# Two attention layers on one core: value products of two steps issued together, and a pool of eight for the weights

## The chip, the core and the metric

One core of a Trainium2 chip runs the whole program. The metric is device time in microseconds; lower is better. Engines are named as in the profile: PE is TensorE (matrix products), DVE is VectorE, ACT is ScalarE, POOL is GpSimd and SP issues most DMAs. Matrix products are written to PSUM, eight banks of 512 float32 columns on 128 partitions; the other engines read them there.

## The reference

The input x has two images of 256 channels and 64 x 64 positions, so 4096 tokens each. Two layers follow each other.

Layer 0 (4 heads of 16):

```python
xn = layernorm over channels(x) * norm_w + norm_b
q, k, v = split(einsum('bnc,oc->bno', xn, qkv_w))
attn = softmax(einsum('bhnd,bhmd->bhnm', q, k) * 16 ** -0.5)
dyn = conv2(relu(conv1(x)))                 # one factor for each query
out = einsum('bhnm,bhmd->bhnd', attn * dyn, v)
x = sigmoid(gamma * (out @ out_w.T) + x)
```

Layer 1 (4 heads of 64): queries, keys and values from x by 1 x 1 convolutions with bias, `softmax(q k / 8) v`, an output convolution with bias, plus x. The result is float32.

## The kernel before

**Preparation.** The first stretch of the program normalises x block by block (512 tokens), makes queries and keys as sums of three bf16 parts, the values in float32 (`vs0`, 32 columns for each head, the first of them ones, so that the value product also gives the sum of the weights) and `dyn`. Its tiles lie in pools (`own_prep`) that are closed before the loop.

**Layer 0's loop.** A unit is one image and a block of 512 queries; there are 16 units of 32 steps (`END0` = 512 steps). A step takes 128 keys against the unit's 512 queries, for 4 heads. The loop variable is t. Every instruction is issued through `seq`, which keeps the program's order on each engine, so the order written in the loop is the order on PE, ACT, DVE and POOL. A step issues, in this order:

- `weigh(t, 0)`: two score products s (L453) for heads 0 and 1, each followed by its exponential (L458, ACT), from a PSUM tile of one bank (`ps2`, three buffers) into half of a weight tile p (128 x 2 x 512 float32 in SBUF);
- `maxima(t + LEAD0, 1)`: two score products a (L407) for the queries of a later step, into a two-bank tile (`ps1`, two buffers), and one DVE reduction over them (L412). `LEAD0` is 35: the maxima of a unit are found while the unit before it is weighed, and are subtracted in the later products by three more rows of the operands;
- `weigh(t, 1)` and `maxima(t + LEAD0, 0)` for heads 2 and 3;
- `gather(t - 1)`: the value products av (L471) of the step before, four products with 32 columns each, one for each head, accumulated over the unit in one bank (`psa`, one buffer). At a unit's last step it also copies that bank to SBUF (L483, ACT);
- what is hung on this step: `fold` and `turn` (the maxima of the next unit are split and put into its queries, steps 28 to 30 of a unit; `turn` borrows a `ps1` tile for `nm`, L434, which ACT copies, L438), `send_sums`, `factor` and `scale_all` (1 over the sums, by way of DRAM), `project` (L555, borrows a `ps1` tile for o) and `add_x` (L560, DVE), `finish` and the loads.

Maxima stop where t + 35 reaches 512. From there on the tile of heads 0 and 1 is a pair from `ps1` with one exponential over both banks (L460), and layer 1's first keys, values and queries are made between the steps.

The weight tile comes from the pool `l0w`, which also holds queries and factors, with four buffers of its tag: two tiles for each step, so two steps. The name `l0p` does not exist. The pool `l0w` is opened ahead of the preparation's pools, so it lies below them.

**Layer 1** follows with its own pools once layer 0's are closed. Nothing in it is touched.

Of the kernel before, what the change touches and what calls it, by code (L numbers as in the profile page):

```python
# [8 lines left out]
F32 = mybir.dt.float32  # L9
# [6 lines left out]
P = 128  # L16
NB = 512
# [15 lines left out]
def conv_attention_kernel(  # L33
# [20 lines left out]
    B, _, N = x.shape  # L54
# [9 lines left out]
    own0 = ExitStack()  # L64
# [3 lines left out]
    l0w = own0.enter_context(tc.tile_pool(name="l0w", bufs=2))  # L68
# [91 lines left out]
    def later_load(t, src):  # L160
        nc.sync.dma_start(out=t, in_=src)
        return t

    def more_constants():

        gam = later_load(
            const.tile([P, 1], F32, tag="gam", name="gam"), gamma.partition_broadcast(P)
        )
        wo0 = const0.tile([P, C], F32, tag="wo0", name="wo0")
        nc.gpsimd.memset(wo0, 0.0)  # L170
        for h in range(H):
            later_load(
                wo0[32 * h + 1 : 32 * h + 1 + D0, :], out_wT[h * D0 : (h + 1) * D0, :]
            )
        return gam, wo0
# [39 lines left out]
    def hung(t, place):  # L215
        for step in extras.pop((t, place), []):
            step()
# [11 lines left out]
    END0 = len(units0) * NM  # L229
# [4 lines left out]
    with own0:  # L234
# [11 lines left out]
            seq(nc.gpsimd.memset(ones_at, 1.0))  # L246

        work, qs0, mxs, pts, avs, dyns, res, facts = {}, {}, {}, {}, {}, {}, {}, {}
        ks0, negs0 = {}, {}

        def bank_two(name):
            return pairs[0].tile([P, 2, NB], F32, tag="two", name=name)
# [145 lines left out]
        def maxima(x, g):  # L398

            u = b, j = units0[x // NM]  # L400
            m, i = divmod(x % NM, PB)
            if u not in mxs:
                mxs[u] = small.tile([P, PB * H, NJ], F32, tag="mx0", name=f"mx0_{b}_{j}")
            ps = bank_two(f"a0_{b}_{j}_{x % NM}_{g}")
            for k in range(2):
                h = 2 * g + k
                seq(nc.tensor.matmul(  # L407
                    ps[:, k, :], qs0[u][:RQ, h, bass.ts(i, P)], ks0[b, m][:RQ, h, :],
                    start=True, stop=True,
                ))  # L410
            h = i * H + 2 * g
            seq(nc.vector.tensor_reduce(mxs[u][:, h : h + 2, m], ps, AX.X, ALU.max))  # L412
# [27 lines left out]
        def weigh(t, g):  # L440
            u = b, j = units0[t // NM]
            m = t % NM
            pt = l0w.tile([P, 2, NB], F32, tag="p", bufs=4, name=f"p0_{b}_{j}_{m}_{g}")
            late = t + LEAD0 >= END0 and g == 0
            if late:
                two = bank_two(f"s0_{b}_{j}_{m}")
            for k in range(2):
                h = 2 * g + k
                if late:
                    ps = two[:, k, :]  # L450
                else:
                    ps = ps2.tile([P, NB], F32, tag="s", name=f"s0_{b}_{j}_{m}_{h}")
                seq(nc.tensor.matmul(  # L453
                    ps, ks0[b, m // PB][:RS, h, bass.ts(m % PB, P)], qs0[u][:RS, h, :],
                    start=True, stop=True,
                ))
                if not late:
                    seq(nc.scalar.activation(pt[:, k, :], ps, AF.Exp, scale=D0**-0.5))  # L458
            if late:
                seq(nc.scalar.activation(pt, two, AF.Exp, scale=D0**-0.5))  # L460
            pts[t, g] = pt

        def gather(t):


            u = b, j = units0[t // NM]
            m = t % NM
            if m == 0:
                avs[u] = psa.tile([P, NB], F32, tag="av", name=f"av0_{b}_{j}")
            for h in range(H):  # L470
                seq(nc.tensor.matmul(  # L471
                    avs[u][32 * h : 32 * h + 32, :],
                    vs0[b][:, m, 32 * h : 32 * h + 32],
                    pts[t, h // 2][:, h % 2, :],
                    start=(m == 0),
                    stop=(m == NM - 1),
                    skip_group_check=True,
                ))
            pts.pop((t, 0))
            pts.pop((t, 1))  # L480
            if m == NM - 1:
                a = l0w.tile([P, NB], F32, tag="avs", name=f"avs0_{b}_{j}")
                seq(nc.scalar.copy(a, avs[u]))  # L483
                avs[u] = a
# [118 lines left out]
        for n in range(len(blocks) + 3):  # L603
# [37 lines left out]
            if old is not None:  # L641
                prep_product(*old)
                prep_split(*old)
                b, j = old
# [20 lines left out]
        ps2 = own_psum.enter_context(tc.tile_pool(name="ps2", bufs=3, space=PSUM))  # L665
        psa = own_psum.enter_context(tc.tile_pool(name="psa", bufs=1, space=PSUM))
        pairs[0] = ps1
        gam, wo0 = more_constants()


# [83 lines left out]
        for t in range(-LEAD0 + NM, max(t for t, _ in extras) + 1):  # L754
            ahead = t + LEAD0
            hung(t, "start")
            if 0 <= t < END0:
                weigh(t, 0)
            if ahead < END0:
                maxima(ahead, 1)  # L760
            hung(t, "middle")
            if 0 <= t < END0:
                weigh(t, 1)
            if ahead < END0:
                maxima(ahead, 0)
            if 0 <= t - 1 < END0:
                gather(t - 1)
            hung(t, "end")
        assert not extras
# [23 lines left out]
    with (  # L793
# [468 lines left out]
        for n, u in enumerate(units):  # L1262
            b, g, j = u
# [142 lines left out]
        for t in range(max(t for t, _ in extras) + 1):  # L1406
            inside, behind = 0 <= t < END, 0 <= t - LAG < END
            pair = (2 * t, 2 * t + 1)
            scores = [score(pair[0])] if inside else []
            if 0 <= t - LAG - 1 < END:  # L1410
                weigh(pair[1] - 2 * LAG - 2)
            hung(t, "start")
            hung(t, "between")
            if inside:
                scores.append(score(pair[1]))
            hung(t, "early")
            if inside:
                keep(pair[0], scores[0])
            hung(t, "kept")
            if behind:  # L1420
                shift(pair[0] - 2 * LAG)
                weigh(pair[0] - 2 * LAG)
            hung(t, "early end")
            if inside:
                keep(pair[1], scores[1])
            if 0 <= t - LAG - 1 < END:
                for c in pair:
                    gather(c - 2 * LAG - 2)
                    if c - 2 * LAG - 2 == 2 * END - 2:
                        keep_late(1)  # L1430
            hung(t, "late")
            hung(t, "late end")
            if behind:
                shift(pair[1] - 2 * LAG)
            hung(t, "end")
# [67 lines left out]
```

## Time and profile before

| | |
|---|---|
| median of 3 runs | 4342.19 us (4340.53 to 4343.92) |
| profiled execution | 4343.31 us, span 4341.5 us, mean granted PE clock 0.99 |
| busy in the span | PE 95%, DVE 86%, ACT 79%, POOL 60% |
| layer 0's steps with value products | first av at 252.5 us, last at 1758.4 us |

The windows view gives busy time of each engine in a stretch, with the number of instructions in brackets. In the timeline each row has the start, the time until the last of the merged instructions ends, the engine, line, operation, output and inputs, and in square brackets the engine's idle time ahead of it with what ended that. A PE row's end is modelled and overlaps the next row, so the pace of PE is read from start to start. The value products are float32; a step's four of them leave eight records.

### The profile page before, as it was taken

How to read it: one execution, taken by the hardware profiler on the slowest of the kernel's cores; microseconds unless marked ns; L12 is line 12 of the kernel's file. 1: busy time of each engine (PE TensorE's matmuls, PEld its weight loads, DVE VectorE, ACT ScalarE, POOL GpSimd, SP SyncE). 2: the span in 40 equal slices, each digit the busy share in tenths (PEclk: the TensorE clock that was granted, in tenths of full speed). 3: DMA queues.
4: the chain of work that ended last, by engine and by line, in shares of the span. 5: the costliest groups of instructions: out<-in, count | busy, mean ns of one | idle time of the engine just before them, and what ended most of it. 6: DMA issues, size and time to landing. Idle time of an engine off the chain costs nothing. (4 is left out here: it accounts for less than half of the span.)

```text
span 4341.5 us, 56781 instructions
## 1 busy us (share of the span) xinstructions
PE 4120.8 (95%) x20650; PEld 1348.3 (31%) x20650; DVE 3725.2 (86%) x3417; ACT 3422.0 (79%) x4616; POOL 2584.8 (60%) x1456
## 2 busy tenths in 40 slices
PE   6899999999999999899999999999999999999998
PEld 3433333333333333333333333333333333222322
DVE  5778888888888883599999999999999999999997
ACT  2257777777777777698889888898898888988885
POOL 6600000010000000299999999999999999999995
PEclk8889999999999999999999999999999999999999
DMA  5400000010000002111112111112211112211213
GB/s 145 117 19 22 25 24 17 17 37 21 17 21 19 14 13 71 59 35 40 40 34 66 50 42 38 33 41 69 54 36 37 40 45 59 60 40 42 52 40 117
DMA packets 237521, 191.63 MB, mean 44 GB/s; under 512 B 155700, under 2 KB 168820, under 8 KB 237240
## 3 DMA queue, kind: packets, MB, share of 16 engines
q1 hardware_dynamic: 235384, 187.40, 16.2%
q8 instruction: 162, 2.65, 0.3%
q14 instruction: 119, 0.97, 0.1%
q10 hardware_dynamic: 1856, 0.59, 0.1%
HBM read 136.55 MB, written 51.38 MB: 43 GB/s over the span
## 5 line engine op out<-in xcount | busy, mean ns | idle before, releaser
L1027 POOL TENSOR_TENSOR acc<-acc,raw 128x1024 f32<-128x1024 f32 x821 | 1949.6, 2375 | 60.7 <-ACT raw L1015 9.3
L412 DVE TENSOR_REDUCE mx<-a 128x2 f32<-128x1024 f32 x1024 | 1209.1, 1221 | 252.5 <-PE a L407 248.2
L458 ACT ACTIVATE p<-s 128x512 f32<-128x512 f32 x1978 | 1023.4, 604 | 349.6 <-PE s L453 348.8
L931 DVE TENSOR_TENSOR rmax<-s,rmax 128x1024 f32<-128x1024 f32 x960 | 1172.7, 1222 | 139.9 <-PE s L914 128.6
L914 PE MATMUL s<-q,k 64*128 64x512 f32 x4096 | 1114.7, 636 | 105.7 <-ACT raw L932 101.3
L932 ACT COPY raw<-s 128x1024 f32<-128x1024 f32 x1024 | 1036.6, 1012 | 206.8 <-DVE rmax L931 109.8
L1003 DVE TENSOR_TENSOR raw<-raw,shift 128x1024 f32<-128x1024 f32 x961 | 1164.3, 1213 | 3.9 <-ACT shift L985 2.4
L1015 ACT ACTIVATE raw<-raw 128x1024 f32<-128x1024 f32 x1024 | 1086.6, 1062 | 78.7 <-DVE raw L1003 47.8
L1056 PE MATMUL av<-raw,v 128*64 128x512 f32 x4096 | 1008.9, 608 | 4.0 <-ACT raw L1015 2.5
L453 PE MATMUL s<-q,k 99*128 99x512 bf16 x2048 | 616.6, 381 | 15.4 <-ACT p L458 14.7
L407 PE MATMUL a<-k,q 96*128 96x512 bf16 x2048 | 612.0, 382 | 10.7 <-DVE mx L412 8.8
L471 PE MATMUL av<-p,v 128*32 128x512 f32 x4096 | 546.2, 605 | 0.2 <-ACT avs L483 0.2
L914 PEld LDWEIGHTS s<-q,k 64*128 64x128 f32 x4096 | 311.7, 185 | 707.2 <-ACT raw L932 525.6
L1056 PEld LDWEIGHTS av<-raw,v 128*64 128x64 f32 x4096 | 243.0, 136 | 651.8 <-issue 455.1
L453 PEld LDWEIGHTS <-k 99*128 99x128 bf16 x2048 | 160.8, 97 | 516.9 <-issue 390.5
L570 POOL TENSOR_SCALAR res<-res 128x1024 f32<-128x1024 f32 x16 | 16.7, 1044 | 498.1 <-ACT res L569 498.1
L407 PEld LDWEIGHTS <-q 96*128 96x128 bf16 x2048 | 200.8, 98 | 285.6 <-issue 56.5
L422 POOL CAST part<-neg 128x16 bf16<-128x16 f32 x16 | 3.4, 211 | 446.7 <-PE a L407 274.3
L519 POOL TENSOR_TENSOR f<-f,dyn 128x16 f32<-128x16 f32 x15 | 3.3, 221 | 371.8 <-DVE f L518 371.8
L1025 POOL TENSOR_TENSOR acc<-raw,raw 128x1024 f32<-128x1024 f32 x64 | 152.4, 2382 | 54.0 <-ACT raw L1015 54.0
L992 POOL TENSOR_TENSOR raw<-raw,row 128x1024 f32<-128x1024 f32 x63 | 152.2, 2417 | 39.0 <-DMA row<-neg 39.0
L471 PEld LDWEIGHTS av<-p,v 128*32 128x32 f32 x4096 | 80.9, 108 | 218.2 <-issue 210.2
(345 smaller groups left out, 2101.9 us busy)
## 6 DMA issues: line engine op xcount, KB each, us to landing
row<-neg SPq DMA_DIRECT2D x64, 512.0 KB
x<-in_x_dram SPq DMA_DIRECT2D x16, 512.0 KB
res<-in_x_dram SPq DMA_DIRECT2D x16, 512.0 KB
x<-res SPq DMA_DIRECT2D x16, 512.0 KB
att<-rows SPq DMA_DIRECT2D x62, 128.0 KB
kd<-part SPq DMA_DIRECT2D x96, 64.0 KB
qd<-part SPq DMA_DIRECT2D x96, 64.0 KB
k<-kd SPq DMA_DIRECT2D x16, 384.0 KB
```

The lines of the kernel that those rows point to most:

```text
L407: seq(nc.tensor.matmul(ps[:, k, :], qs0[u][:RQ, h, bass.ts(i, P)], ks0[b, m][:RQ, h, :], start=True, stop=True,))
L412: seq(nc.vector.tensor_reduce(mxs[u][:, h : h + 2, m], ps, AX.X, ALU.max))
L453: seq(nc.tensor.matmul(ps, ks0[b, m // PB][:RS, h, bass.ts(m % PB, P)], qs0[u][:RS, h, :], start=True, stop=True,))
L458: seq(nc.scalar.activation(pt[:, k, :], ps, AF.Exp, scale=D0**-0.5))
L471: seq(nc.tensor.matmul(avs[u][32 * h : 32 * h + 32, :], vs0[b][:, m, 32 * h : 32 * h + 32], pts[t, h // 2][:, h % 2, :], start=(m == 0), s ...
L914: seq(nc.tensor.matmul(ps[:, k, :], ks[b, g, m // PB][r, bass.ts(m % PB, P)], qs1[u][r, :], start=True, stop=True,))
L931: seq(nc.vector.tensor_tensor(rmax[u, n], ps, before, ALU.max))
L932: seq(nc.scalar.copy(raw, ps))
L1003: seq(nc.vector.tensor_tensor(raws[t], raws[t], shifts[u, t % NM // GS], ALU.add))
L1015: seq(nc.scalar.activation(p, p, AF.Exp, scale=D1**-0.5))
L1027: seq(nc.gpsimd.tensor_tensor(accs[u, n], accs[u, n], p, ALU.add))
L1056: seq(nc.tensor.matmul(avs1[u, n][k * D1 : (k + 1) * D1, :], v[:, m % PB, k, :], raws[t][:, k, :], start=(m % GS == 0), stop=(m % GS == GS ...
```

## The change

`gather` is no longer called in every step. In every second step (t even) it is called twice, for t - 2 and for t - 1, so that the value products of two steps stand behind each other in PE's queue; the odd steps have none. All 512 are still issued, the last two at t = 512.

Since the weights of two steps now wait for their products while a third step's are made, the weight tiles move out of `l0w` (four buffers) into a pool `l0p` of their own with eight. It is opened after the preparation's pools are closed, so it lies where their tiles were. `l0w` and what lies behind it get smaller and move down by the four buffers.

```diff
-        ks0, negs0 = {}, {}
+        ks0, negs0, l0p = {}, {}, []
...
-            pt = l0w.tile([P, 2, NB], F32, tag="p", bufs=4, name=f"p0_{b}_{j}_{m}_{g}")
+            pt = l0p[0].tile([P, 2, NB], F32, tag="p", name=f"p0_{b}_{j}_{m}_{g}")
...
         pairs[0] = ps1
+        l0p.append(own0.enter_context(tc.tile_pool(name="l0p", bufs=8)))
         gam, wo0 = more_constants()
...
             if ahead < END0:
                 maxima(ahead, 0)
-            if 0 <= t - 1 < END0:
+            if t % 2 == 0 and 0 <= t - 2 < END0:
+                gather(t - 2)
                 gather(t - 1)
             hung(t, "end")
```

## The prediction, made before the changed kernel was run

> **What bounds the kernel now.** I read the page first, then the windows view of layer 0, the timeline of a few of its steps, the waits, and last some stretches where a step ran otherwise.
>
> ```profile
> PE 4120.8 (95%) x20650; PEld 1348.3 (31%) x20650; DVE 3725.2 (86%) x3417; ACT 3422.0 (79%) x4616; POOL 2584.8 (60%) x1456
> ```
>
> 95% for TensorE mixes two layers. The change touches only layer 0, so its stretch is what counts:
>
> ```profile
> core 0: us, PE busy (x) PEld busy (x) DVE busy (x) ACT busy (x) POOL busy (x), PEclk, DMA share, GB/s
> 700.00:790.00 90.00, 88.89 (x505) 27.57 (x502) 73.39 (x65) 65.84 (x126) 3.40 (x7) 1.00 0.07 20
> ```
>
> Of 90 us TensorE is busy 88.9 at a granted clock of 1.00, VectorE 73.4, ScalarE 65.8. TensorE sets the pace; VectorE has a fifth of its time to spare. One whole step, with the loads left out:
>
> ```profile
> 1205.27 0.60 PE L453 MATMUL s<-q,k 99*128 99x512 bf16 x2
> 1205.69 2.06 ACT L458 ACTIVATE p<-s 128x512 f32<-128x512 f32 x4 [0.77 <-PE s L453]
> 1205.71 0.60 PE L407 MATMUL a<-k,q 96*128 96x512 bf16 x2
> 1206.14 0.59 PE L453 MATMUL s<-q,k 99*128 99x512 bf16 x2
> 1206.34 2.36 DVE L412 TENSOR_REDUCE mx<-a 128x2 f32<-128x1024 f32 x2 [0.47 <-PE a L407]
> 1206.58 0.59 PE L407 MATMUL a<-k,q 96*128 96x512 bf16 x2
> 1207.10 1.06 PE L471 MATMUL av<-p,v 128*32 128x512 f32 x8
> 1208.10 0.60 PE L453 MATMUL s<-q,k 99*128 99x512 bf16 x2
> ```
>
> First column start, second duration. A step is 1208.10 - 1205.27 = 2.83 us: four bf16 pairs (s, a, s, a) at 0.43 to 0.44 from start to start, then 0.52 from the last a to av (0.43 for the pair, 0.09 for the turn to av) and 1.00 from av to the next s. VectorE does its two reduces in 2.36 us and then stands 0.47, waiting for the next a: this idle time and its place, across the value products, is what I follow below.
>
> ```profile
> DVE mx L412 <- PE a L407: 195.0, 379, 1.2
> PE s L453 <- ACT p L458: 12.6, 24, 0.5
> ```
>
> So between 500 and 1800 us VectorE waits for TensorE, and TensorE almost never waits; no row for "PE a waits for DVE mx" appears.
>
> **What the change saves.** The value products of a step are 8 records, four 32-column products at once, in two waves. I need the time of a wave when more follow. The end of the loop has two gathers in a row; short windows of the timeline show where waves start:
>
> ```profile
> 1756.17 0.64 PE L471 MATMUL av<-p,v 128*32 128x512 f32 x4
> 1756.62 1.03 PE L471 MATMUL av<-p,v 128*32 128x512 f32 x6
> 1757.05 1.03 PE L471 MATMUL av<-p,v 128*32 128x512 f32 x5
> ```
>
> 0.45 and 0.43 us. A gather alone costs 0.09 + 1.00 = 1.09, of which two waves are 0.88, so 0.21 us is turning to 32-column float32 work and back. Two behind each other cost 0.09 + 1.00 + 0.88 = 1.97 instead of 2.18. If nothing else were late, two steps would go from 5.66 to 5.45 us.
>
> The Trainium skill states the same effect ("TensorEngine Tiling (Array Packing)", Key Properties): a change of tiling mode drains the array. It gives no price; by this rule alone the sum would be 238 x -0.21 = -50 us. The same page, under PSUM Bottleneck, speaks against it: tiling speeds up TensorE, not the emptying of PSUM, and the copy may become the bottleneck; by that rule the saving goes into a wait. The rows decide between them.
>
> **What the change takes.** After the change TensorE runs s, a, s, a, s, a, s, a without a break and then spends 1.97 us in which it feeds neither VectorE nor ScalarE. The a tiles come from ps1, which has two buffers: a third a must wait for the end of the reduce two before it. Today the gather after every second a gives VectorE that time. The loop's first steps, before there is anything to gather, show what happens without it:
>
> ```profile
> 250.70 3.49 DVE L412 TENSOR_REDUCE mx<-a 128x2 f32<-128x1024 f32 x3 [0.20 <-PE a L407]
> 250.94 0.59 PE L407 MATMUL a<-k,q 96*128 96x512 bf16 x2
> 251.37 0.59 PE L453 MATMUL s<-q,k 99*128 99x512 bf16 x2
> 251.98 0.59 PE L407 MATMUL a<-k,q 96*128 96x512 bf16 x2
> 252.50 1.06 PE L471 MATMUL av<-p,v 128*32 128x512 f32 x8
> ```
>
> The s pair of 251.37 leaves TensorE free at 251.80, but a starts at 251.98: the first of the three reduces ends at 250.70 + 1.22 = 251.92 (1.22 is the mean of this group), and a follows 0.05 later. That wait is small here and comes once. In the new order it comes in every second step, and the chain closes on itself. From the start of a1, the first a after a double gather:
> - 0.63 until its reduce starts (1205.71 to 1206.34);
> - 2.36 for the reduces of a1 and a2, back to back (a2 was there long before);
> - 0.05 until a4 may start in a2's tile. TensorE would be there at 2.8 (a1 and a2 0.87 with their s pairs each, a3 held until a1's reduce is over at 0.63 + 1.22 + 0.05 = 1.90, then a3 and s 0.87), so it waits 0.2 to 0.3, after some 0.2 at a3;
> - 1.52 from a4 to the next s as today (1206.58 to 1208.10), plus two waves, 0.88: 2.40;
> - 0.44 for the s pair ahead of the next a1.
>
> Sum 5.88 us for two steps, against 5.66: **0.22 slower**, though TensorE works 0.21 less. VectorE works 4 x 1.14 = 4.56 of the 5.88 and now idles in one piece of about 1.3, because two reduces of stored work last 2.4 us and the gap from a4 to the next a1's reduce is 2.40 + 0.44 + 0.63 = 3.47.
>
> Maxima run in steps 0 to 476 (they are 35 ahead of 512), 238 pairs: 238 x 0.22 = +52 us. Bounds: the waves at 0.43 or 0.45 give 0.86 to 0.90, the handover 0.03 to 0.07, the turn back to s 0.02 either way: 5.84 to 5.92, so +43 to +62.
>
> **Extras of a unit.** A unit of 32 steps takes 95.1 us today (the starts of the avs copies), 4.4 more than 32 x 2.83: two turns of the maxima and two projections, each of which borrows one of the two ps1 tiles. A projection is 0.95 of TensorE now (o at 963.43, s at 964.39), and the 0.75 us add on VectorE is hidden. On a VectorE chain that add counts, and the tile comes back only behind it; I put a projection at 1.1 to 1.5 and leave a turn as it is (its 1.00 us ScalarE copy holds it up today, with a wait of 0.52). Bounds for a unit: -0.5 (the turn's wait disappears in the other stall) to +1.0 (two more such waits). I take +0.5, nearest to the one 0.52 row: 15 x 0.5 = +7, with -7 to +15.
>
> **The last 35 steps** have no maxima and take 1.97 us each. ScalarE works about 1.88 of that (an exponential of a pair and two single ones, starts 0.92, 0.48, 0.48 apart), so of the 0.21 per pair little is left: -1, bounds -4 and +2.
>
> **Weights' own pool.** Six tiles are alive at most with two gathers pending, so eight buffers make nobody wait. The pool lies where the preparation's tiles were, and the first exponential gains waits for that area's DMAs, GpSimd, VectorE and TensorE; the built order shows them, and the same DMA waits on the first value product. In the trace the last stores out of that area are issued at 237.3 on SP's queue, and the first exponential starts at 247.99, so they lie hidden; if that cover failed, it would be a few us once. All other queues, SP's and GpSimd's included, keep their order, and the exponentials have more slack than before: at 8 x 0.48 = 3.8 of 5.88 us, off the chain with three s banks. Zero, at most +1.
>
> Sum: 52 + 7 - 1 = +58. The profiled execution took 4343.31 us (span 4341.5), 1.1 above the median of 4342.19; so 4342.2 + 58 = **4400 us**.
>
> **Rivals.** *Faster, because the a tiles don't hold TensorE up.* Place: the wait of a4 for a2's reduce. It decides if the handover chain is under 5.66, that is, if the two reduces took 0.22 less than 2.36, or a third tile were there. Then either TensorE's own 5.45 counts, 238 x -0.21 = -50 us, 4292, or the next limit does: the s banks, where from the first s to the last 0.42 + 4 x 0.48 + 0.60 + 0.05 = 2.99, then 0.22 + 0.43 + 1.97 = 5.61, -12 us, 4330. For it: VectorE's spare fifth. Against: the row at 251.98, and a tile count the change leaves alone. 7%.
>
> *Much slower, by the clock.* TensorE would idle 5.88 - 5.45 = 0.43 of each 5.88. In the VectorE-bound stretch from 231 to 250 us the a pairs stood at half pace (starts 0.43 apart for one matmul, where 0.22 is usual). If a tenth of the loop ran so, its 140 us would need up to 5.45 more per pair: about +125 us, over 4500. Against: the 90 us windows hold turns with a 0.52 stall and still show 1.00. 4%. The skill warns of it ("TensorE: Matmul & The Clock Gate", A second HAM failure mode): short idling between matmul groups while PSUM banks cycle can throttle the clock. No loop row here shows it at 92% busy.
>
> *No change.* The saved turns and the stall cancel: that needs 5.66 exactly, 3%. That the gathers aren't paired is no case: the built order has av records in sixteens.
>
> **Numbers.** About 0.2% (9 us) is what a measurement of this kernel can tell from no change. Main case 86%. Its low end: 43 - 7 - 4 = +32, 4374; its high end 62 + 15 + 2 + 1 = +80, 4422. Slower by over 0.2%: 86 + 4 = 90%; within 3%; faster 7%. The range leaves out the rivals, 14%.
>
> **What would show it.** Right: in a steady stretch of layer 0 two steps of 5.8 to 5.9 us; PE's a waiting for DVE's mx, twice per two steps, some 0.2 to 0.3 each; VectorE's idle time in one piece of 1.2 to 1.4; av in sixteens of 1.85 to 1.95; granted clock 1.00; layer 1 as long as before. Wrong: no wait of a on mx with two steps at 5.45 to 5.6, or a clock below 1.00.

## The result and the profile after

The changed kernel takes 4403.99 us (median of 4 runs, 4400.8 to 4407.27) against 4341.36 us for the kernel before in the same comparison: ratio 1.0144, 95% interval 1.0127 to 1.0162: 1.4% slower. The forecast was 4400, with 4374 to 4422.

All of it lies in layer 0. The copy of the last unit's av ends the loop's value products: it starts at 1759.08 us before and at 1819.14 after, 60.06 later. From layer 1's first copy to the end of the trace it is 2567.8 us before and 2567.6 after. The profiled span grew by 59.8, from 4341.5 to 4401.3.

The windows view of the stretch shown in the prediction, now of the changed kernel (same columns):

```profile
700.00:790.00 90.00, 86.46 (x484) 28.92 (x486) 69.57 (x62) 63.43 (x124) 3.41 (x7) 1.00 0.07 20
```

Every engine does less per microsecond: TensorE 86.5 instead of 88.9, VectorE 69.6 instead of 73.4, ScalarE 63.4 instead of 65.8. No engine has become the bound; they wait for each other. The granted clock is still 1.00. The busy time of TensorE, whose ends are modelled, hides most of its waiting; starts show it. Two steady steps in the timeline, loads left out:

```profile
1245.46 0.61 PE L453 MATMUL s<-q,k 99*128 99x512 bf16 x2
1245.89 4.03 ACT L458 ACTIVATE p<-s 128x512 f32<-128x512 f32 x8 [1.60 <-PE s L453]
1245.91 0.60 PE L407 MATMUL a<-k,q 96*128 96x512 bf16 x2
1246.34 0.60 PE L453 MATMUL s<-q,k 99*128 99x512 bf16 x2
1246.54 4.62 DVE L412 TENSOR_REDUCE mx<-a 128x2 f32<-128x1024 f32 x4 [1.25 <-PE a L407]
1246.78 0.60 PE L407 MATMUL a<-k,q 96*128 96x512 bf16 x2
1247.21 0.69 PE L453 MATMUL s<-q,k 99*128 99x512 bf16 x2
1247.82 0.59 PE L407 MATMUL a<-k,q 96*128 96x512 bf16 x2
1248.25 0.62 PE L453 MATMUL s<-q,k 99*128 99x512 bf16 x2
1248.95 0.59 PE L407 MATMUL a<-k,q 96*128 96x512 bf16 x2
1249.47 1.92 PE L471 MATMUL av<-p,v 128*32 128x512 f32 x16
1251.33 0.61 PE L453 MATMUL s<-q,k 99*128 99x512 bf16 x2
```

Two steps are 1251.33 - 1245.46 = 5.87 us, before 5.66. The first two a stand 0.87 apart, the third 1.04 behind the second, the fourth 1.13 behind the third: the last two wait about 0.17 and 0.26. VectorE runs its four reduces in one piece of 4.62 and then idles 1.25. Its second reduce ends at 1246.54 + 1.14 + 1.22 = 1248.90, and the fourth a starts 0.05 later, in the tile that this reduce gave back.

The saving is there as well. The group of the value products in the page, first of the kernel before, then of the changed one:

```profile
L471 PE MATMUL av<-p,v 128*32 128x512 f32 x4096 | 546.2, 605 | 0.2 <-ACT avs L483 0.2
```

```profile
L471 PE MATMUL av<-p,v 128*32 128x512 f32 x4096 | 493.4, 598 | 0.0
```

53 us less busy time, 0.21 for each of 256 pairs, as worked out; and the kernel is 60 us slower. Starts, which are not modelled, say slightly more: from the first av to the next s it is 1251.33 - 1249.47 = 1.86 us for two gathers, where one takes 1.00; so the second costs 0.86, and a pair of gathers saves 0.23.

### The profile page after: what moved, and what is told of

The parts are those of the page before. It is cut to its first block, busy times and chain, and to the rows that moved or that the text cites. A ratio compares the mean times of both kernels' runs of the same rounds, so it can differ in the third digit from the quotient of the medians.

```text
span 4401.3 us, 56783 instructions
## 1 busy us (share of the span) xinstructions
PE 4141.5 (94%) x20650; PEld 1391.5 (32%) x20650; DVE 3707.1 (84%) x3417; ACT 3404.2 (77%) x4616; POOL 2584.9 (59%) x1456
## 5 line engine op out<-in xcount | busy, mean ns | idle before, releaser
L412 DVE TENSOR_REDUCE mx<-a 128x2 f32<-128x1024 f32 x1024 | 1192.5, 1219 | 344.9 <-PE a L407 341.7
L458 ACT ACTIVATE p<-s 128x512 f32<-128x512 f32 x1978 | 1004.5, 623 | 409.8 <-PE s L453 409.1
L453 PE MATMUL s<-q,k 99*128 99x512 bf16 x2048 | 643.3, 380 | 27.7 <-ACT p L458 26.9
L471 PE MATMUL av<-p,v 128*32 128x512 f32 x4096 | 493.4, 598 | 0.0
L453 PEld LDWEIGHTS <-k 99*128 99x128 bf16 x2048 | 177.3, 97 | 397.1 <-issue 223.3
L471 PEld LDWEIGHTS av<-p,v 128*32 128x32 f32 x4096 | 107.1, 109 | 265.9 <-issue 264.5
```

What stands on the lines that cost most here:

```text
L453: seq(nc.tensor.matmul(ps, ks0[b, m // PB][:RS, h, bass.ts(m % PB, P)], qs0[u][:RS, h, :], start=True, stop=True,))
L471: seq(nc.tensor.matmul(avs[u][32 * h : 32 * h + 32, :], vs0[b][:, m, 32 * h : 32 * h + 32], pts[t, h // 2][:, h % 2, :], start=(m == 0), s ...
```

## The experiments

The theory, A in the expectations: the two ps1 tiles are handed back too late across a double gather, that is, the two gathers of a pair behind each other. Its rivals, B there: in the first run the pool, in the others a double gather that is slow in itself. A chain is a row of steps that wait for each other: products fill a tile, another engine empties it, and the next products need it back. The table puts the runs side by side; "two steps" is the distance of the first av of two neighbouring pairs in a steady stretch of the trace, "unit" the distance of two avs copies.

| kernel | median us | ratio to before, 95% | two steps | unit |
|---|---|---|---|---|
| before | 4341 to 4343 | | 5.67 | 95.1 |
| changed | 4403.99 | 1.0144 (1.0127 to 1.0162) | 5.87 | 99.2 |
| pool only | 4343.63 | 1.0004 (0.9995 to 1.0013) | 5.67 | 95.1 |
| changed, half reduce | 4344.07 | 1.0005 (0.9996 to 1.0015) | 5.63 | 95.3 |
| before, half reduce | 4339.68 | 0.9995 (0.9986 to 1.0005) | 5.67 | 95.1 |
| changed, a first behind the pair | 4436.80 | 1.0219 (1.0204 to 1.0234) | 6.06 | 101.45 |
| changed, one-bank tiles | 4334.43 | 0.9985 (0.9976 to 0.9995) | 5.63 | 94.8 |
| the same, s and a alternating | 4293.52 | 0.9889 (0.9872 to 0.9905) | 5.45 | 92.2 |
| before, one-bank tiles, alternating | 4331.97 | 0.9981 (0.9972 to 0.9990) | 5.69 | 94.5 |
| alternating, ScalarE's extras ahead of the pair | 4278.51 | 0.9857 (0.9842 to 0.9872) | 5.45 | 91.1 |
| changed, tanh moved | 4392.26 | 1.0117 (1.0100 to 1.0133) | 5.87 | 98.5 |

**The pool alone.** The weights in the pool of eight, a gather in every step.

```diff
-            if t % 2 == 0 and 0 <= t - 2 < END0:
-                gather(t - 2)
+            if 0 <= t - 1 < END0:
                 gather(t - 1)
```

> The weight tiles in their own pool of eight, but a gather in every step as before. Theory A (the loss comes from the two ps1 tiles that VectorE hands back too late across a double gather): the pool costs nothing, two steps stay at 5.66 us, 4341 us within 5. Rival B (the pool's place, its new waits or the longer life of the weight tiles take part in the loss): above 4350.

4343.63 us, no difference, and the same 2.83 us for a steady step. The pool has no part in the loss; pairing alone makes it.

**Half a reduce, in the changed kernel and in the one before.**

```diff
-            seq(nc.vector.tensor_reduce(mxs[u][:, h : h + 2, m], ps, AX.X, ALU.max))
+            seq(nc.vector.tensor_reduce(mxs[u][:, h : h + 2, m], ps[:, :, : NB // 2], AX.X, ALU.max))
```

> The changed kernel, with each maximum taken over the first 256 of 512 keys of a product only (the other half is left out of the maximum; the softmax itself keeps all keys). A reduce becomes about 0.69 us long, 0.60 apart. Theory A: a no longer waits for mx; what is late next is the three s banks, 5.63 us for two steps by the same walk, so 4404 - 238 x 0.24 and the extras of the units, about 4335 us (4325 to 4345). Rival B (the double gather itself is slower than its waves, by clock or PSUM writes): VectorE's length changes nothing, 4404. Rival C (nothing at all is late next): 5.45 us, 4290.

> The same shortened maximum in the kernel before (half of the keys is left out of the maximum). Theory A: TensorE sets the pace there, VectorE only idles longer, 4341 us within 5. If VectorE had a share in the pace of the kernel before, it would be faster by more than 10 us.

In the changed kernel 60 us go away by a shorter reduce on VectorE alone; in the kernel before the same edit does nothing that can be measured. So the double gather isn't slow in itself, and in the paired order VectorE's length decides, though VectorE is less busy than before. Two steps fall to 5.63 us, exactly the next limit that was named. Its timeline:

```profile
1225.45 0.71 PE L453 MATMUL s<-q,k 99*128 99x512 bf16 x2
1225.65 0.69 DVE L412 TENSOR_REDUCE mx<-a 128x2 f32<-128x512 f32 x1 [0.26 <-PE a L407]
1225.99 0.60 PE L407 MATMUL a<-k,q 96*128 96x512 bf16 x2
```

Here it is the second s of the pair that comes late: s from 1225.45 to a at 1225.99 is 0.54 where a pair takes 0.43, while VectorE idles 0.26 and waits for a. With three banks in ps2 this eighth s needs the bank of the fifth: in the trace the fifth exponential ends at 1225.73, and the eighth s starts 0.05 later, at 1225.78. The total was expected at 4335 and came out at 4344, at the edge of its range: the unit's extras cost as much as in the changed kernel (95.3 - 16 x 5.63 = 5.2 us, before 95.1 - 16 x 5.67 = 4.4), and a part of the gain I had expected from them didn't come. That is taken up below.

**a ahead of s behind the pair.** In odd steps the first a stands ahead of the first s pair.

```diff
+            if t % 2 == 1 and ahead < END0:
+                maxima(ahead, 1)
             if 0 <= t < END0:
                 weigh(t, 0)
-            if ahead < END0:
+            if t % 2 == 0 and ahead < END0:
                 maxima(ahead, 1)
```

> The changed kernel, but in odd steps (those right behind a double gather) the first a stands ahead of the first s pair, so four s follow each other. Theory A in its full form (two hand-back chains, one for a and one for s): the chain of a falls by 0.44 to 5.45, but the fourth s in a row must wait for the first exponential (three s banks), and the chain of s becomes the longer: 6.07 us for two steps, about 4404 + 238 x 0.19 = 4450 us (4430 to 4465), with s waiting for p. If only the tiles of a mattered: 5.45 us, about 4300. If neither did: 4404.

4436.80 us; two steps 6.06. This shortens the chain of a by an s pair and still costs 33 us more than the change, because four s now follow each other and there are three banks for them:

```profile
1205.30 0.81 PE L453 MATMUL s<-q,k 99*128 99x512 bf16 x3
1205.72 2.06 ACT L458 ACTIVATE p<-s 128x512 f32<-128x512 f32 x4 [2.04 <-PE s L453]
1206.36 0.38 PE L453 MATMUL s<-q,k 99*128 99x512 bf16 x1 [0.25 <-ACT p L458]
```

The first exponential ends about 0.60 after 1205.72, and the fourth s starts at 1206.36. Two chains of tiles that are handed back, one for a and one for s, set the time of a pair of steps.

**The same four banks as four tiles.** ps1 gets four tiles of one bank; each head's a has its own tile and its own reduce. The copies of the turned maxima and the last units' pairs are split in the same way.

```diff
-            ps = bank_two(f"a0_{b}_{j}_{x % NM}_{g}")
-            for k in range(2):
+            for k in range(2) if only is None else (only,):
                 h = 2 * g + k
+                ps = bank(f"a0_{b}_{j}_{x % NM}_{h}")
...
-            h = i * H + 2 * g
-            seq(nc.vector.tensor_reduce(mxs[u][:, h : h + 2, m], ps, AX.X, ALU.max))
+                h = i * H + h
+                seq(nc.vector.tensor_reduce(
+                    mxs[u][:, h : h + 1, m], ps.unsqueeze(1), AX.X, ALU.max
+                ))
...
-        ps1 = own_psum.enter_context(tc.tile_pool(name="ps1", bufs=2, space=PSUM))
+        ps1 = own_psum.enter_context(tc.tile_pool(name="ps1", bufs=4, space=PSUM))
```

> The changed kernel with the same four PSUM banks of ps1 cut into four tiles of one bank, each with one head's a and its own reduce (0.69 us, 0.60 apart as the runs with half a reduce showed), so a bank is handed back after one head. Theory A: the chain of a falls from 5.87 to about 5.6, the chain of s (three banks) stays at 5.63: two steps 5.63 us, and the unit's extras cost 0.8 more than before, as in the run with the half reduce: about 4345 us (4335 to 4355). Rival B (the paired gather itself is slow): 4404.

4334.43 us: all keys are in the maximum, VectorE does more work than in the changed kernel, and the loss is gone. What counted was when a bank comes back. Two steps are 5.63 as expected. The total is just below the 4335 to 4355 that were expected: a unit's extras cost 4.7 us and not the 5.2 of the half reduce (a unit takes 94.8 instead of 95.3), and units 14 and 15, with their pairs split, are shorter too (the last unit 84.6 us instead of 85.8).

**Alternating s and a**, on top of it, and the control without pairing.

```diff
-            if 0 <= t < END0:
-                weigh(t, 0)
-            if ahead < END0:
-                maxima(ahead, 1)
-            hung(t, "middle")
-            if 0 <= t < END0:
-                weigh(t, 1)
-            if ahead < END0:
-                maxima(ahead, 0)
+            for g in range(2):
+                if g == 1:
+                    hung(t, "middle")
+                for k in range(2):
+                    if 0 <= t < END0:
+                        weigh(t, g, k)
+                    if ahead < END0:
+                        maxima(ahead, 1 - g, k)
```

> As the run before, and s and a alternate singly (s, a, s, a) where pairs stood. Theory A: behind the last s and ahead of the first s stands only one a, so the chain of s falls to 5.20 + 0.22 = 5.41 and that of a to about 5.40; TensorE's own 5.44 is the longest: 238 x -0.22 = -53 us, less about 13 for the extras, about 4302 us (4288 to 4318). If alternating brings its own cost on TensorE (more switches between the two products), 4340 or more.

> Control: one-bank tiles and alternating in the kernel before, gathers in every step. Theory A: TensorE sets the pace, 2.83 us for a step whatever the tiles: 4342 us within 8. If the gain of the run before came from the tiles or the order alone, it shows here too, about 4300.

4293.52 us, 1.1% faster than the kernel before, and two steps of 5.45 us: TensorE's own sum, the one that the change would give if nothing else were late. Its windows view, and from its timeline VectorE's reduces and one pair's end and start:

```profile
700.00:790.00 90.00, 88.88 (x516) 31.36 (x513) 78.69 (x131) 67.13 (x132) 3.40 (x7) 1.00 0.07 20
```

```profile
1241.49 4.87 DVE L409 TENSOR_REDUCE mx<-a 128x1 f32<-128x512 f32 x8 [0.58 <-PE a L404]
1244.13 0.38 PE L404 MATMUL a<-k,q 96*128 96x512 bf16 x1
1244.44 1.92 PE L467 MATMUL av<-p,v 128*32 128x512 f32 x16
1246.29 0.39 PE L453 MATMUL s<-q,k 99*128 99x512 bf16 x1
1246.52 0.38 PE L404 MATMUL a<-k,q 96*128 96x512 bf16 x1
```

The s and a products start 0.22 apart without a gap, VectorE's eight reduces lie in one piece of 4.87 us, and the first a follows the double gather after one s. The control is 4331.97 us, just below the 4342 within 8 that were expected: 9 us come from the tiles and the order without any pairing. They don't come from the steady steps, which are a little longer (2.85 instead of 2.83), but from the two steps with the turns of a unit (3.58 instead of 3.97, their copies being split) and the step with the copy of av (3.05 before, here as long as the others). So of 48 us, 38 need the pairing.

**ScalarE's extras.** Two runs ask why the unit's extras cost more in the paired order. In the changed kernel the pair of steps in which a finished unit's tanh is issued takes 6.56 us; its timeline:

```profile
999.40 1.08 ACT L569 ACTIVATE res<-res 128x1024 f32<-128x1024 f32 x1
999.84 0.38 PE L453 MATMUL s<-q,k 99*128 99x512 bf16 x1
1000.35 2.09 ACT L458 ACTIVATE p<-s 128x512 f32<-128x512 f32 x4
1001.02 0.38 PE L453 MATMUL s<-q,k 99*128 99x512 bf16 x1 [0.80 <-ACT p L458]
```

The tanh stands in ScalarE's queue ahead of four exponentials, and the next s waits 0.80 for a bank. The move puts it ahead of the next double gather, in which ScalarE has nothing to do:

```diff
-            at(t1 + 4, "end", lambda u=u: finish(u))
+            if u == units0[-1]:
+                at(t1 + 4, "end", lambda u=u: finish(u))
+            else:
+                at(t1 + 5, "gap", lambda u=u: finish(u))
...
+            hung(t, "gap")
             if t % 2 == 0 and 0 <= t - 2 < END0:
                 gather(t - 2)
```

> The changed kernel with one move: the tanh of a finished unit (ScalarE, 1.08 us) is issued ahead of the next double gather instead of behind the odd step's maxima. In the trace after, the two steps with the tanh take 6.56 us instead of 5.87, with s waiting for p. If the tanh in the chain of s is what makes that pair long, it becomes 5.87 and 14 x 0.69 = 10 us return: about 4394 us (4388 to 4400). If that pair is long for the projections' tiles, nothing returns: 4404.

4392.26 us; that pair of steps is 5.87 like the others, a unit takes 98.5 us instead of 99.2, and 0.7 x 14 = 10 us return. The same move in the alternating kernel, with both turns of the maxima ahead of the gather as well:

```diff
-            at(t0 - 3, "end", lambda u=u: turn(u, 0))
-            at(t0 - 2, "end", lambda u=u: turn(u, 1))
+            at(t0 - 2, "gap", lambda u=u: turn(u, 0))
+            at(t0 - 2, "gap", lambda u=u: turn(u, 1))
```

> As the alternating paired kernel, with ScalarE's extra work (the two copies of the turned maxima and the tanh of a finished unit) issued ahead of a double gather, where ScalarE has nothing to do. If the unit's extras cost more in the paired order because that work falls into the chain of s, most of the 13 us returns: about 4290 us (4280 to 4305). If they cost more for another reason: as the run without the move, 4302.

4278.51 us, just below the 4280 to 4305 that were expected and 15 less than without the move: the pair with the tanh falls from 6.35 to 5.45, the two with the turns from 6.63 + 6.40 to 7.19 + 5.65; together 1.1 for a unit, 14 units. This is the fastest kernel of the study: 0.9857 of the time before, 0.9842 to 0.9872.

## Why the prediction was right, and where it was off

- **The saving**, 0.21 us for a pair: right; 53 us of busy time are gone, or 0.23 a pair by starts. That the alternating kernel runs at just the 5.45 of the forecast is in part luck: its own control takes 5.69 without pairing, so there the pairing saves 0.24, and alternating takes 0.03 back. The Trainium skill's "TensorEngine Tiling (Array Packing)" says under Key Properties that a change of tiling mode drains TensorE. The 0.21 agrees with that but doesn't show it by itself, since the products change from bf16 to float32 at the same place. Under PSUM Bottleneck it says that a quicker TensorE may leave the emptying of PSUM as the bottleneck. That is what the half reduce shows here, though the tiles that come back late are those of a, whose products are not tiled.
- **The chain of a**: right in its place and nearly in size. By the rows after: 0.63 to the first reduce, 2.36 for two, 0.05 to the fourth a, 2.38 to the next s (2.40 forecast), 0.45 to the next a: 5.87 instead of 5.88. 238 pairs make 238 x 0.20 = 48 us (52 forecast, since two steps before are 5.67 rather than 5.66). That this chain makes the loss is shown by the half reduce and by the four one-bank tiles, each of which takes the loss away without touching the gathers. The bounds given for it, 5.84 to 5.92, are narrower than their three terms, which add up to 5.82 to 5.94; 5.87 lies in both.
- **The extras of a unit**: the mis-sized term, inside its bounds. +0.5 was forecast, +0.9 measured (99.2 - 16 x 5.87 = 5.3 against 4.4), some 13 us instead of 7. I had looked for it in the projections' tiles on VectorE, and they did become dearer: the two cost 7.07 + 7.00 - 2 x 5.87 = 2.3 us instead of 1.9, near the low end of the 1.1 to 1.5 each that I gave. What I left out is the tanh: I had called the exponentials "off the chain". They are, but only by 5.87 - 5.63 = 0.24 us, and the tanh of 1.08 is longer than that. It costs 0.7 in each unit, against 0.04 before (2.87 instead of 2.83 in its step), and the run that moves it shows this. I left out a gain too: the step with the copy of av took 3.05 before, 0.22 more than others, and in the changed kernel its pair takes 5.87 like the rest. That a third of the tanh was paid back in this way is luck. Why the projections cost more wasn't tried by itself.
- **The last 35 steps**: the last unit is 0.4 us shorter (86.24 to 85.80); -1 was forecast. The three terms together make 48 + 13 - 0.4 = 61 us, and the trace shows 60.
- **The pool**: nothing, as forecast.
- **Rivals.** That the a tiles don't hold TensorE up: refuted by the half reduce. Its second part, s banks as the next limit, was right: 5.61 was forecast, 5.63 measured. The clock stayed at 1.00 although TensorE stood still for about 7% of the time (0.43 of 5.87); the throttling of which the Trainium skill's "TensorE: Matmul & The Clock Gate" warns under A second HAM failure mode was not seen with pauses this short (0.17 and 0.26 in a steady pair).
- **What should have shown it.** The two steps, VectorE's one idle piece, av in sixteens at 1.92 and the clock came as written. One sign failed: the waits view has no row for a waiting for mx in the steady steps. The gaps of 0.17 and 0.26 lie under the modelled ends of the s products ahead of them, and only starts show them.

## What to carry to other kernels

Grouping TensorE's work saves the turns between two kinds of products, but it also makes a hole in what the other engines get; before grouping, add up the time from the last tile ahead of the hole to the first one behind it, and see whether the tiles in PSUM hold that much work. Where they don't, hand the same banks back in smaller pieces and alternate the products, so that each chain sees only one foreign product on either side of the hole; here that turned 1.4% slower into 1.1% faster. And work of an engine that was free of charge (a tanh in slack) is to be priced anew in the new order; put into the hole it is free again.

## What the runs showed of the hardware

- The second gather of a pair, two waves of four 32-column float32 products, costs 0.86 us from start to start, and one alone 1.09 with its turns. So going from bf16 products over all columns to these and back costs about 0.23 us a time (0.21 by busy time, whose ends are modelled).
- A reduce over 512 columns of PSUM takes 0.69 us, over 1024 1.22, so two halves in a row cost VectorE about 5% more (8 in 4.87 us against 4 in 4.62), and that was worth paying.
- Alternating bf16 products of s and a in place of pairs makes a step 0.013 us longer (2.846 instead of 2.833 in the control, whose tiles are cut as well).
- VectorE and ScalarE both became less busy in the run that got slower, and VectorE's length still decided: how busy an engine is did not tell whether it was on the path.
